# Reading Wv by rows and placing the expert weights' load behind the last normed rows' writes, in a gated attention and mixture-of-experts kernel

## The chip, the cores and the metric

The kernel runs on one core of a Trainium2 chip. The metric is the time of one execution in microseconds on the device. The kernel before takes 576.2 us in the median of three runs (575.97 to 576.66). A profiled execution of it took 577.64 us, of which 575.9 us lie between its first and its last instruction; all rows of the profile come from that execution.

## The reference, cut to what matters

The input x has 2 batches of 1024 tokens with 512 features, all in float32. Every row is normalised (layer norm without weights) to xn. Attention and a mixture of experts both start from xn, and their results are multiplied:

```
xn  = (x - mean) / sqrt(var + 1e-5)
q, k, v = split(xn @ w_qkv.T + b_qkv)            # 512 features each
s   = softmax(q @ k.T / sqrt(512)) @ v @ w_out.T + b_out
logits = xn @ router_w + router_b                 # 8 experts
top 2 experts per token, softmax over the two logits
f   = sum over the two: weight * silu(xn @ expert_w[e] + expert_b[e])
y   = xn + f @ proj_w + proj_b
g   = silu(norm_w * y / sqrt(mean(y*y) + 1e-6))
out = x + s * g
```

The host hands `w_qkv` and `w_out` over transposed, so that `w_qkvT` has a row for each input feature (512 rows) and 1536 columns; the last 512 columns are Wv.

## The kernel before, in words

Tokens are handled in 16 tiles of 128 rows. The features of a row are not kept in their natural order. VectorE transposes 32 by 32 blocks, and the kernel lays x, the weights and the normed rows out so that such block transposes are enough. The contraction over 512 features runs in four steps of 128, and step j takes the features q*128 + j*32 + b for q in 0..3 and b in 0..31. A weight that is contracted with xn must have its rows in the same order.

The work goes through these stages.

1. **Head.** Wv and Wo are multiplied into one matrix, so that values come out already projected: `wv_in` (Wv in four chunks of 128 rows) is transposed chunk by chunk on TensorE (`turn_wv`, L394), copied by VectorE into `wvT`, and multiplied with `wo` (`product_vo`, L403) for two halves n of the output columns and four row groups hc. Results land in `rwvo`, which also holds the eight columns of the router weights (`rw`). In between, statistics of the first x tiles are taken (`parts`, `means`, `variances`), x is normed by ScalarE in place (`norm`), transposed by VectorE (`turn_x`) and written to DRAM as `xn_d`, two tiles at a time in four DMAs (`store`, L381). `turn_w` transposes the blocks of Wq (`wZ[0]`) and of Wk (`wZ[1]`). `hold` (L220) issues matmuls on a constant tile whose result nobody reads.
2. **Values.** For t from 0 to 15, `value_half` multiplies xnT with `rwvo` (the `pv` matmuls, L457); each step of the loop also norms, stores or takes statistics of later tiles, and does one part of the weights' work. Logits come out of the same matmuls.
3. **Routing.** After the last tile the pools of the first stages are closed (`close(ln_guard)`), and their room goes to the routing tiles (`hsel`, `tsel`, `lsel`, L677 to L698) and to the expert biases `eb`. The two experts of each token are found, tokens are counted by expert, and 39 slots of 128 rows get their lists of tokens (`tok`). Meanwhile TensorE multiplies Wq and Wk (`product`) and the queries (`queries`, the `pq` matmuls, L549). It does `queries(0)` ahead of the token matmuls `ptok` (L706) and `queries(1)` to `queries(3)` behind them.
4. **Experts.** A pipeline over 39 slots: `gather` (POOL, an indirect DMA, L782) fetches a slot's rows of `xn_d` seven slots ahead, `put_s` writes them to DRAM in another layout (`xs`), `take_s` reads them back (`sz`), `turn_s` transposes them on VectorE (`gT`), and `expert` multiplies them with the expert's weights out of `ew` (the `ph` matmuls, L808). The expert's number is only known at run time, so the matmul depends on the whole tile `ew` (8 MB). Results are written by ACT's queue to `ho_d`.
5. **Attention and the gate**, in pairs of tiles, to the end.

The order on each engine is the written order: `keep_order()` ties every instruction to the one before it on its engine. DMAs are issued by SP in that order too, a few by ACT and POOL. In the built program every DMA that SP or ACT issues waits for the one eight DMAs earlier to have landed. A DMA of SP that has to wait keeps back everything behind it on SP.

The head's DMAs stand on SP in this order: Wv chunks 0 and 1, the first half of Wo, Wv chunks 2 and 3, x tiles 0 and 1, the second half of Wo, `wZ[0]`, x tiles 2 and 3, x tiles 4 to 15, `wZ[1]`. ACT issues the biases `bqkv` and then the router weights (four DMAs of 4 KB). At step t = 12 of the values' loop the `raw` pool is closed, and the 32 DMAs of `ew` are issued at once. Step t = 13 issues `store(14)`, the write of tiles 14 and 15, so it stands behind `ew` on SP.

Of the kernel before, what the change touches and what calls it, by code (L numbers as in the profile page):

```python
# [10 lines left out]
FP = mybir.dt.float32  # L11
# [9 lines left out]
P = 128  # L21
# [6 lines left out]
def kernel(  # L28
# [17 lines left out]
    B, S, H = hidden.shape  # L46
    E = router_w.shape[1]
    KC = H // P
# [18 lines left out]
    def pool(name, bufs=1, side="left", **where):  # L67
        guard = tc.tile_pool(name=name, bufs=bufs, side=side, reuse_waits="tile", **where)
        return guard, guard.__enter__()
# [3 lines left out]
    def close(guard):  # L73
        guard.__exit__(None, None, None)
# [25 lines left out]
    pe, dve, act, gps, sp = nc.tensor, nc.vector, nc.scalar, nc.gpsimd, nc.sync  # L100
# [8 lines left out]
    QP = P // 4  # L109
# [22 lines left out]
    def turn_w(dst, z):  # L132

        for r in range(KC):
            dve.transpose(
                dst.rearrange("p j (i q a) -> p i j q a", i=4, q=4)[:, :, :, r, :],
                z[:, ts(r, 4), :].rearrange("p i (j b) -> p i j b", b=QP),
            )
# [22 lines left out]
    raw_guard, raw = pool("raw", side="right")  # L161
# [12 lines left out]
    def load_x(t, n):  # L174
        for q in range(4):
            sp.dma_start(
                x[ts(q, QP), ds(t, n)].rearrange("p t i f -> p (t i) f"),
                xr_d[ds(t * P, n * P), ts(q, P)].rearrange("(n a) f -> a n f", a=QP),
            )

    wv_in = raw.tile([P, KC, H], FP, name="wv_in")
# [3 lines left out]
    bqk = const.tile([P, 2, KC], FP, name="bqk")  # L185

    def load_wv(c):
        sp.dma_start(
            wv_in[:, c, :],
            w_qkvT.rearrange("(q j b) o -> j q b o", q=4, b=QP)[c][:, :, ts(2, H)],  # L190
        )

    def load_wo(n):
        sp.dma_start(
            wo[:, :, ts(n, HH)], w_outT[:, ts(n, HH)].rearrange("(c p) h -> p c h", p=P)
        )

    act.dma_start(bqkv, b_qkv.rearrange("p (i c) -> p i c", i=3))
    load_wv(0)
    load_wv(1)  # L200
    load_wo(0)
    for c in range(2, KC):
        load_wv(c)
    load_x(0, 2)
    load_wo(1)
    spread(sp, wZ[0], w_qkvT[:, ts(0, H)])
    load_x(2, 2)
    for q in range(4):
        act.dma_start(
            rw[ts(q, QP), :, 0:E], router_w[ts(q, P), :].rearrange("(j b) e -> b j e", b=QP)  # L210
        )
    for t in range(4, NT, 4):
# [7 lines left out]
    def hold(n):  # L220
        ps = ps_mm.tile([P, 512], FP, tag="mm", name="hold")
        for _ in range(n):
            pe.matmul(ps[:, : 2 * P], lhsT=idle[:, 0:P], rhs=idle, start=True, stop=True)
# [92 lines left out]
    def weighted(w_, bias, name):  # L316

        s_ = raw.tile([P, H], FP, tag="s", name=name, bufs=3)
        for c in range(KC):
            b_ = bias[:, c : c + 1]  # L320
            if c:
                dve.scalar_tensor_tensor(s_, w_[:, c, :], b_, s_, ALU.mult, ALU.add)
            else:
                dve.tensor_scalar(s_, w_[:, c, :], b_, None, ALU.mult)
            yield s_
# [10 lines left out]
    def parts(t):  # L336
        for i in range(4):
            dve.bn_stats(st[:, t, i].rearrange("p h k -> p (h k)"), x[:, t, i, :])
# [10 lines left out]
    def means(t, n):  # L349
        g_ = ds(4 * t, 4 * n)  # L350
        at_ = st.rearrange("p t i h k -> p (t i) h k")[:, g_]
        dve.tensor_reduce(mean[:, g_], across(at_[:, :, :, 1], f"pmean{t}"), AX.X, ALU.add)
        dve.tensor_tensor(
            dev[:, g_],
            at_[:, :, :, 1],
            mean[:, g_].unsqueeze(2).to_broadcast([P, 4 * n, 2]),
            ALU.subtract,
        )
        dve.tensor_tensor(dev[:, g_], dev[:, g_], dev[:, g_], ALU.mult)
        dve.scalar_tensor_tensor(  # L360
            dev[:, g_], at_[:, :, :, 2], 8.0 / H, dev[:, g_], ALU.mult, ALU.add
        )

    def variances(t, n):
        g_ = ds(4 * t, 4 * n)
        dve.tensor_reduce(var[:, g_], across(dev[:, g_], f"pvar{t}"), AX.X, ALU.add)
        act.activation(std[:, g_], var[:, g_], AF.Sqrt, bias=ln_eps)
        dve.reciprocal(rstd[:, g_], std[:, g_])
        dve.scalar_tensor_tensor(
            shift[:, g_], mean[:, g_], -1.0, rstd[:, g_], ALU.mult, ALU.mult  # L370
        )

    def norm(t):
        for i in range(4):
            n = 4 * t + i
            act.activation(  # L376
                x[:, t, i, :], x[:, t, i, :], AF.Identity,
                bias=shift[:, n : n + 1], scale=rstd[:, n : n + 1],
            )

    def store(t):  # L381

        for q in range(4):
            sp.dma_start(
                xn_d[ds(t * P, 2 * P), ts(q, P)].rearrange("(n a) f -> a n f", a=QP),
                x[ts(q, QP), ds(t, 2)].rearrange("p t i f -> p (t i) f"),
            )

    def turn_x(t):
        turn(xnT[t // ST][:, :, ts(t % ST, P)], x[:, t], "(i a)")  # L390

    wvT = {}

    def turn_wv(c):  # L394
        ps = ps_mm.tile([P, 512], FP, tag="mm", name=f"wvt{c}").rearrange(
            "p (o f) -> p o f", o=KC
        )
        for oc in range(KC):
            pe.transpose(ps[:, oc, :], wv_in[:, c, ts(oc, P)], ident)
        wvT[c] = raw.tile([P, KC, P], FP, name=f"wvT{c}")  # L400
        dve.tensor_copy(wvT[c], ps)

    def product_vo(n, hc):  # L403
        at_, size = halves[n]
        ps = ps_mm.tile([P, 512], FP, tag="mm", name=f"pvo{hc}_{n}")
        for c in range(KC):
            pe.matmul(
                ps[:, :size],
                lhsT=wvT[hc][:, c, :],
                rhs=wo[:, c, ts(n, HH)],  # L410
                start=(c == 0),
                stop=(c == KC - 1),
            )
        act.copy(rwvo[:, hc, at_ : at_ + size], ps[:, :size])

    hold(12)
    turn_wv(0)
    hold(6)
    turn_wv(1)
    product_vo(0, 0)  # L420
    turn_wv(2)
    parts(0)
    parts(1)
    product_vo(0, 1)
    turn_wv(3)
    product_vo(0, 2)
    means(0, 2)
    product_vo(0, 3)
# [23 lines left out]
    def value_half(t, n):  # L452
        if t not in pvs:
            pvs[t] = ps_big.tile([P, 2, 512], FP, tag="big", name=f"pv{t}")
        cols = (ds(0, HH + E1), ds(HH + E1, HH))[n]
        for c in range(KC):
            pe.matmul(  # L457
                pvs[t][:, n, : HH + E1 * (1 - n)],
                lhsT=xnT[t // ST][:, c, ts(t % ST, P)],
                rhs=rwvo[:, c, cols],  # L460
                start=(c == 0),
                stop=(c == KC - 1),
            )

    def keep_values(t):
        pv = pvs.pop(t)
        dst = vo[t // ST][:, t % ST, :].rearrange("p (n f) -> p n f", n=2)
        act.copy(dst, pv[:, :, 0:HH])
        act.copy(lg1[:, t, :], pv[:, 0, HH : HH + E1])
# [25 lines left out]
    for t in range(2, NT):  # L495
        if 2 < t < NT - 1:
            turn_x(t + 1)
        value_half(t, 1)
        keep_values(t - 1)
        if t in (2, 5, 9):  # L500
            first = {2: 4, 5: 8, 9: 12}[t]
            means(first, 4)
        value_half(t, 0)
        if t in (2, 5, 9):
            variances(first, 4)
        if t + 2 < NT:
            norm(t + 2)
            if t % 2:
                store(t + 1)
        if 3 <= t < 7:  # L510
            parts(2 * t + 2)
            parts(2 * t + 3)
        if t == 2:
            gps.dma_start(bo, b_out.partition_broadcast(P))
        if t == 8:
            turn_w(wqkT[:, KC:], wZ[1])
        if t == 9:
            *_, sk_ = weighted(wqkT[:, KC:], bqk[:, 0], "sk")
        if t == 10:

            *_, vb = weighted(wo, bqkv[:, 2], "vb")
        if t == 11:
            dve.tensor_copy(u, columns(sk_, "pu"))
        if t == 12:
            pvb = ps_mm.tile([P, 512], FP, tag="mm", name="pvb")
            pe.matmul(pvb, lhsT=ones, rhs=vb, start=True, stop=True)
            dve.tensor_tensor(bo, pvb, bo, ALU.add)
            close(raw_guard)
            ew_guard, ewp = pool("ew", side="right")
            ew = ewp.tile([P, E, KC, H], FP, name="ew")  # L530
            for e in range(E):
                for q in range(4):
                    sp.dma_start(
                        ew[ts(q, QP), e],
                        expert_w[e, ts(q, P), :].rearrange("(j b) f -> b j f", b=QP),
                    )
# [159 lines left out]
    for g in range(2 * NT // LG):  # L696
# [7 lines left out]
        for j in range(LG):  # L704
# [3 lines left out]
                lhsT=lsel[:, j, :],  # L708
# [522 lines left out]
    for k in range(NP):  # L1231
# [43 lines left out]
        o = attend(k)  # L1275
# [81 lines left out]
```

## Time and profile before

| what | us |
|---|---|
| median of three runs | 576.2 (575.97 to 576.66) |
| profiled execution | 577.64 |
| its span | 575.9 |
| TensorE busy | 537.6 |
| VectorE busy | 310.7 |
| POOL busy | 215.7 |
| ScalarE busy | 167.5 |
| first `pv` matmuls with the logits' columns (L457) | 44.64 |
| first expert matmul (L808) | 171.66 |
| mean granted TensorE clock | 0.97 |

Times of events count from the span's start. A row of the chain of work that ended last gives start, length, engine, what was written and read, and its line. A row of stretches gives the stretch, its length, the busy time of TensorE's matmuls, TensorE's weight loads, VectorE, ScalarE and POOL (with counts of instructions), then the granted TensorE clock, the mean busy share of the 16 DMA engines, and what they moved in GB/s. A row of waits gives who waited, for whom, total, times and longest.

### The profile page before, as it was taken

Reading aid. Unit: us, or ns where it says so; the run is one execution under the profiler, and the core shown is the slowest. Engines: PE = TensorE matmul, PEld = TensorE weight load, DVE = VectorE, ACT = ScalarE, POOL = GpSimd, SP = SyncE. Lnnn points to the kernel's source line nnn. Section 1 sums busy time; section 2 is a strip of 40 time slices with the busy share of each in tenths; the row PEclk is TensorE's granted clock in tenths of the full one; section 3 lists DMA queues with packets and bytes.
Section 4 is the critical chain, followed back from the end, with each engine's and each line's share of the span. In section 5 each row is a group of like instructions: output and inputs, shape, how many; then the busy total and the mean of one; then the engine's idle time right before and its main releaser. Section 6 shows DMA issues by size and latency. Waiting matters only on the chain.

```text
span 575.9 us, 5914 instructions
## 1 busy us (share of the span) xinstructions
PE 537.6 (93%) x1758; PEld 327.1 (57%) x1758; DVE 310.7 (54%) x565; ACT 167.5 (29%) x316; POOL 215.7 (37%) x238
## 2 busy tenths in 40 slices
PE   5789999980899999999999999999999999999997
PEld 3568878630444444444446666675674847475486
DVE  0264763403403333433376846638479595868686
ACT  0143754210012111121134152242342425252340
POOL 6000000000342457632202744524819857484542
PEclk9997999995699999999999999999999999999999
DMA  5898225999498999999737792362532827365522
GB/s 122 181 213 162 71 71 117 211 211 252 132 325 254 274 334 349 303 303 302 220 143 242 232 314 70 105 242 73 184 146 74 306 94 275 128 219 204 179 92 75
DMA packets 95857, 112.38 MB, mean 195 GB/s; under 512 B 7248, under 2 KB 65744, under 8 KB 95696
## 3 DMA queue, kind: packets, MB, share of 16 engines
q1 hardware_dynamic: 83696, 82.86, 50.5%
q0 software_dynamic: 5792, 18.88, 10.4%
q10 hardware_dynamic: 6336, 10.25, 4.8%
q8 instruction: 15, 0.25, 0.2%
q14 instruction: 18, 0.15, 0.1%
HBM read 70.54 MB, written 41.42 MB: 194 GB/s over the span
## 4 chain that ended last, share of the span: by engine, by line
PE 76%; DMA 13%; DVE 7%; issue 2%; ACT 0%; SPq 0%; DVEq 0%
PE ph L808 19%; PE so L1141 16%; PE pp L1070 13%; PE po L1007 10%; PE pv L457 7%; DMA ew<-in_L_ffn_expert_w_dram 6%; PE pq L549 4%; PE pr L568 4%; DMA wv_in<-in_L_attn_w_qkv_dram 3%; PE sc L1051 2%; DMA wZ<-in_L_attn_w_qkv_dram 1%; DMA xn_d<-x 1%; DMA x<-_attn_hidden_states_dram 1%; DVE lsel L698 1%; DVE sc L1076 1%
## 5 line engine op out<-in xcount | busy, mean ns | idle before, releaser
L808 PE MATMUL ph<-ew,gT 128*128 x280 | 120.3, 592 | 0.0
L782 POOL DMA_INDIRECT xg<-xn_d,tok x39 | 37.2, 954 | 199.7 <-DVE npast L727 138.3
L808 PEld LDWEIGHTS ph<-ew,gT 128*128 128x128 f32 x280 | 53.2, 190 | 67.0 <-issue 67.0
L834 DVE TENSOR_TENSOR h<-ph,eb 128x512 f32<-128x512 f32 x39 | 26.9, 689 | 83.9 <-issue 55.3
L457 PE MATMUL pv<-rwvo,xnT 128*128 128x256 f32 (+1 forms) x256 | 62.3, 400 | 1.3 <-DVE xnT L120 1.0
L457 PEld LDWEIGHTS pv<-rwvo,xnT 128*128 128x128 f32 x256 | 49.5, 197 | 10.8 <-ACT x L376 1.4
L837 ACT ACTIVATE h<-h 128x512 f32<-128x512 f32 x39 | 24.6, 631 | 96.5 <-DVE h L834 96.5
L1007 PE MATMUL po<-pw,ct 128*128 128x512 f32 x112 | 49.2, 592 | 0.0
L1038 ACT ACTIVATE pr<-sc,nm 128x1024 f32<-128x1024 f32 x16 | 18.3, 1144 | 90.8 <-DVE nm L1035 89.1
L969 POOL DMA_INDIRECT hg<-ho_d,posi_m x32 | 31.7, 990 | 33.0 <-DMA ho_d<-h 22.3
L1148 DVE TENSOR_TENSOR o<-so,o 128x256 f32<-128x256 f32 x49 | 20.0, 421 | 39.2 <-PE so L1141 22.5
L1070 PE MATMUL pp<-xnT,qT 128*128 128x512 f32 x84 | 39.5, 592 | 0.0
L1186 POOL TENSOR_TENSOR o<-o,base 128x512 f32<-128x512 f32 x14 | 20.6, 1491 | 48.9 <-DVE o L1151 48.0
L1141 PE MATMUL so<-vo,pT 128*128 128x256 f32 x168 | 38.5, 379 | 0.0
L1141 PEld LDWEIGHTS so<-vo,pT 128*128 128x128 f32 x168 | 31.9, 190 | 7.3 <-issue 2.6
L1007 PEld LDWEIGHTS po<-pw,ct 128*128 128x128 f32 x112 | 21.3, 190 | 25.5 <-issue 25.4
L1076 DVE TENSOR_TENSOR sc<-pp,sc 128x512 f32<-128x512 f32 x49 | 31.6, 679 | 5.2 <-PE pp L1070 5.2
L549 PE MATMUL pq<-xnT,wqk 128*128 128x512 f32 x64 | 30.6, 636 | 0.0
L120 DVE STREAM_TRANSPOSE gT<-sz 128x512 f32<-128x512 f32 x39 | 27.4, 702 | 4.3 <-DMA sz<-xs 4.3
L568 PE MATMUL pr<-xnT,wqk 128*128 128x256 f32 x128 | 28.8, 381 | 0.9 <-DVE sc L1076 0.9
L120 DVE STREAM_TRANSPOSE pT<-pz 128x1024 f32<-128x1024 f32 x14 | 28.1, 2007 | 0.0
L568 PEld LDWEIGHTS pr<-xnT,wqk 128*128 128x128 f32 x128 | 24.2, 190 | 6.6 <-DVE sc L1076 2.2
(223 smaller groups left out, 792.3 us busy)
## 6 DMA issues: line engine op xcount, KB each, us to landing
xs<-xg SPq DMA_DIRECT2D x39, 256.0 KB
sz<-xs SPq DMA_DIRECT2D x39, 256.0 KB
ho_d<-h ACTq DMA_DIRECT2D x39, 256.0 KB
ew<-in_L_ffn_expert_w_dram SPq DMA_DIRECT2D x32, 256.0 KB
ps<-pr SPq DMA_DIRECT2D x16, 512.0 KB
pz<-ps SPq DMA_DIRECT2D x16, 512.0 KB
xn_d<-x SPq DMA_DIRECT2D x32, 128.0 KB
cs<-hg SPq DMA_DIRECT2D x16, 256.0 KB
```

Of the source, the lines that this page charges most:

```text
L120: dve.transpose(dst.rearrange(f"p j {order} -> p i j a", a=QP), z.rearrange("p i (j b) -> p i j b", b=QP),)
L457: pe.matmul(pvs[t][:, n, : HH + E1 * (1 - n)], lhsT=xnT[t // ST][:, c, ts(t % ST, P)], rhs=rwvo[:, c, cols], start=(c == 0), stop=(c == KC ...
L549: pe.matmul(ps[:, half, :], lhsT=wqk[:, c, ts(oc, P)], rhs=xnT[0][:, c, ts(half, 512)], start=(c == 0), stop=(c == KC - 1),)
L568: pe.matmul(ps[:, :PW], lhsT=wqk[:, c, ts(oc, P)], rhs=xnT[1][:, c, ts(k, PW)], start=(c == 0), stop=(c == KC - 1),)
L782: gps.indirect_dma_start(out=xg[s], out_offset=None, in_=xn_d, in_offset=bass.IndirectOffsetOnAxis(ap=tok[:, s : s + 1], axis=0),)
L808: pe.matmul(ph, lhsT=g_[:, c, :], rhs=ew[:, ds(r, 1), c, :].rearrange("p e f -> p (e f)"), start=(c == 0), stop=(c == KC - 1),)
L834: dve.tensor_tensor(h, ph, eb[:, ds(r, 1), :].rearrange("p e f -> p (e f)"), ALU.add)
L969: gps.indirect_dma_start(out=g_, out_offset=None, in_=ho_d, in_offset=bass.IndirectOffsetOnAxis(ap=posi_m[:, n, t : t + 1], axis=0),)
L1007: pe.matmul(po, lhsT=c_[:, c, :], rhs=pw[:, c, :], start=(c == 0), stop=(c == KC - 1))
L1070: pe.matmul(ps, lhsT=l_[:, c, :], rhs=r_[:, c, :], start=(c == 0), stop=(c == KH - 1))
L1076: dve.tensor_tensor(dst, ps, other, ALU.add)
L1141: pe.matmul(ps[:, :w_], lhsT=l_[:, c, :], rhs=r_[:, c, :], start=(c == 0), stop=(c == SK - 1),)
```

## The change

Four things move.

- A chunk of Wv is now 128 neighbouring rows of `w_qkvT`, not four groups of 32 rows. The four chunks are loaded first, ahead of Wo.
- The order of features is made when a transposed chunk is copied: `wvT` becomes one tile, and the copy of chunk c writes runs of 32 elements into it. A product then reads from all four chunks, so all four are transposed ahead of the first product, with four more `hold` matmuls behind them.
- The router weights' four DMAs go from ACT's queue to SP's, behind x tiles 2 and 3.
- The pool of `ew` is opened, and its DMAs are issued, at step t = 13 and not at t = 12. `store(14)` then stands ahead of them on SP.

```diff
     def load_wv(c):
-        sp.dma_start(
-            wv_in[:, c, :],
-            w_qkvT.rearrange("(q j b) o -> j q b o", q=4, b=QP)[c][:, :, ts(2, H)],
-        )
+        sp.dma_start(wv_in[:, c, :], w_qkvT[ts(c, P), ts(2, H)])
...
     act.dma_start(bqkv, b_qkv.rearrange("p (i c) -> p i c", i=3))
-    load_wv(0)
-    load_wv(1)
+    for c in range(KC):
+        load_wv(c)
     load_wo(0)
-    for c in range(2, KC):
-        load_wv(c)
     load_x(0, 2)
     load_wo(1)
     spread(sp, wZ[0], w_qkvT[:, ts(0, H)])
     load_x(2, 2)
     for q in range(4):
-        act.dma_start(
+        sp.dma_start(
             rw[ts(q, QP), :, 0:E], router_w[ts(q, P), :].rearrange("(j b) e -> b j e", b=QP)
         )
...
-    wvT = {}
+
+    wvT = raw.tile([P, KC, KC, 4, QP], FP, name="wvT")
...
-        wvT[c] = raw.tile([P, KC, P], FP, name=f"wvT{c}")
-        dve.tensor_copy(wvT[c], ps)
+        dve.tensor_copy(wvT[:, :, :, c, :], ps.rearrange("p o (j b) -> p o j b", b=QP))
...
-                lhsT=wvT[hc][:, c, :],
+                lhsT=wvT[:, c, hc].rearrange("p q b -> p (q b)"),
...
     turn_wv(0)
     hold(6)
     turn_wv(1)
+    turn_wv(2)
+    turn_wv(3)
+    hold(4)
     product_vo(0, 0)
-    turn_wv(2)
     parts(0)
     parts(1)
     product_vo(0, 1)
-    turn_wv(3)
     product_vo(0, 2)
...
             dve.tensor_tensor(bo, pvb, bo, ALU.add)
             close(raw_guard)
+        if t == 13:
             ew_guard, ewp = pool("ew", side="right")
             ew = ewp.tile([P, E, KC, H], FP, name="ew")
             for e in range(E):
```

## The prediction

> **What bounds the kernel now.** I read the time slices first, then the chain that ended last, then the waits of VectorE, then stretches of the time line with their DMA share and granted clock.
>
> ```profile
> PE   5789999980899999999999999999999999999997
> ...
> PEclk9997999995699999999999999999999999999999
> ```
>
> Each digit is 14.4 us. TensorE is below nine tenths in two places, slices 1 to 3 and slices 9 to 11; behind them it is full. A change in the first 172 us must act in one of these two.
>
> ```profile
> 0.82 7.34 DMA wv_in<-in_L_attn_w_qkv_dram
> ...
> 8.17 12.77 DMA wv_in<-in_L_attn_w_qkv_dram
> 20.96 8.34 DMA wZ<-in_L_attn_w_qkv_dram
> 29.32 5.59 DMA x<-_attn_hidden_states_dram
> ...
> 122.69 9.90 DMA ew<-in_L_ffn_expert_w_dram
> 132.61 5.75 DMA xn_d<-x
> ...
> 138.59 1.50 DVE hsel L677
> ...
> 171.66 109.88 PE ph L808 x256
> ```
>
> In the chain (start, length, what) the head hangs on four loads of Wv, the last landing at 20.96, then on wZ and x. The second gap hangs on the expert weights `ew`, behind which the last four writes of normed rows `xn_d` stand; `hsel` takes the room of x and so waits until these writes have read it.
>
> ```profile
> DVE hsel L677 <- DMA xn_d<-x: 22.1, 1, 22.1
> ...
> PE wvt L399 <- DMA wv_in<-in_L_attn_w_qkv_dram: 7.0, 3, 4.4
> ```
>
> The columns are total, times and longest: VectorE waited 22.1 us at one place, TensorE 7.0 us in three waits.
>
> ```profile
> 2.20:8.20 6.00, 1.72 (x9) 0.91 (x6) 0.00 (x0) 1.28 (x1) 5.04 (x34) 1.00 0.57 125
> 8.20:20.96 12.76, 9.59 (x34) 6.65 (x34) 2.08 (x3) 0.74 (x2) 2.98 (x12) 1.00 0.71 170
> 20.96:44.64 23.68, 19.05 (x87) 15.95 (x87) 12.66 (x45) 8.72 (x21) 0.00 (x0) 0.91 0.97 203
> 96.40:135.50 39.10, 30.43 (x96) 17.32 (x94) 8.65 (x32) 6.81 (x13) 0.00 (x0) 0.92 1.07 213
> 129.20:144.20 15.00, 0.00 (x0) 0.00 (x1) 5.58 (x5) 0.00 (x0) 0.00 (x0) 0.50 0.91 249
> 157.00:171.50 14.50, 14.50 (x37) 6.50 (x36) 1.71 (x4) 2.23 (x2) 6.47 (x7) 1.00 1.02 325
> 171.66:292.00 120.34, 120.34 (x284) 53.25 (x284) 44.60 (x69) 23.85 (x36) 50.13 (x48) 1.00 0.93 289
> ```
>
> The last three columns are clock, DMA share and GB/s. The DMA engines have room while Wv comes (0.57, 0.71) and none while `ew` comes (1.07); the expert loop needs 289 GB/s.
>
> **The change part by part.**
>
> *Wv by rows.* The same 256 KB a chunk and 2 KB a row, but 128 rows in one run and no four groups of 32. The first chunk took 7.34 us; the nearest load of the new shape, `sz` (128 rows of 2 KB), was issued at 157.04 and ended VectorE's wait at 160.46: 3.4 us, beside other traffic. So chunk 0 lands at 0.82 + 3.4 = 4.2, not 8.16.
>
> The Trainium skill (DMA: Bandwidth & Descriptors, section "Why a DMA increments its semaphore by 16 and not by 1") gives a reason: a DMA is spread over the largest count of engines up to 16 that divides the outermost dimension longer than one on both sides, here 4 before and 16 after. The low DMA share beside a late chunk agrees; the sum would be the same by rule and by row.
>
> *Order of the first products.* A product now reads all four copied chunks; before, the first two chunks let the first product start at 12.82. In TensorE's order: transposes of chunk 0 and six hold matmuls, 2.4 us as measured from 8.29 to 10.66; three more chunks at 1.1 us (0.63 at full clock); four hold matmuls, 4/6 of 1.49 = 1.0. From 4.2 that ends at 10.9. The copies write runs of 32 elements in place of 512; no row shows this on the same operation, so I take 0.69 us, the old copy with the same elements and source, under the hold matmuls; at twice that the last copy costs 0.4 (1.4 against 1.0), at less nothing is gained. The first half of Wo is there: 1.57 MB from 2.2 us at 203 GB/s is 9.9. Three products at 1.89 end at 16.6. The first two x tiles: 2.10 MB at 203 GB/s from 2.2 is 12.5, their statistics (1.65) 14.2, so they no longer hold the means (before, VectorE waited for them until 23.20). Mean, fourth product and variance matmul take 2.7 at full clock: 19.3 against 28.41 now. All behind is arithmetic in the same order, 16.2 us to the pv matmuls at 44.64 (the chain goes over the load of x to 34.90, but VectorE's transposes of x ended at 34.96, so the load was not the later one). Next in line is wZ and the second half of Wo: 1.57 MB more, 20.3, wanted at 34.9 - 9.1 = 25.8; then x of tiles 2 and 3, 22.9, wanted at 28. So 9.1 us off. Ends: one product at half clock (3.75, the row at 12.82) leaves 7.2; transposes at full clock give 10.9; x at only 125 GB/s (2.2 to 8.2) leaves 5. I take 9.
>
> *Router weights on SP.* Four issues of together 2.47 us move from ACT's queue to SP's, behind x tiles 2 and 3 and ahead of x tiles 4 to 15 and wZ[1]. ACT's first copy waits for TensorE anyway: nothing. Tiles 4 to 7 land near 22.9 + 5.2 + 2.5 = 30.6, wanted at 45.12 - 9 = 36: covered; without the cover it costs 2.5. The weights themselves land near 26, wanted by 35.
>
> *Expert weights behind the writes.* Times here are still those of before; all slides by the 9. Tile 15 is normed at 96.38; the writes' four issues take 1.83 (as at 87.70), so `ew` is issued from 98.2, not 95.05, behind a wait of SP for ACT that delays nothing but `ew`. The writes land near 101, so `hsel` starts when VectorE is ready, 116.5, not 138.59. Selections (1.5 + 2.9 + 4.6) end by 125.6, under the queries that hold TensorE to 126.83. Token matmuls at full clock 1.5, the rest as measured 1.4: the first gather at 130 against 149.76. TensorE goes on: 126.83 + 1.5 + 7.03 + 0.2 + 13.8 = 149.4.
>
> What is late next: the gathered rows. On SP's queue `xs` stands behind `ew` and `eb`, in order. `ew` 8.39 MB at 213 GB/s: 98.2 + 1.3 + 39.4 = 138.9; four gathers beside it, 1.05 MB at 325, up to 3.2 more: 142.1; `eb` 2.10 MB at 350 GB/s (139 to 145 now): 148.1. First `xs` 149.5, `sz` 3.4 more, transpose 0.7: the first expert at 153.6, TensorE idle 4.2. Now TensorE went idle at 126.83, the clock read 0.50 from 129.2, and the sixteen `pq` matmuls at 148.1 took 9.58 for the 7.03 of those at 119.8: an idle stretch costs 0 to 2.5; I take 1.5. That gives 171.66 - 155.1 = 16.5 us. Ends: no idle time, 22.2; rows late by one more put and take (7.2, from 153.22 to 160.46) with the full clock price make 163.3, so 8.4.
>
> The skill's clock rule (TensorE: Matmul & The Clock Gate, section "Part 1: The HAM clock gate (the 'warmup' mystery)") has the clock halved after an idle window of about 3.4 us and restored after as long a busy one; it speaks against this order, and by it the idle 4.2 would cost up to 1.7. The row of 129.2 agrees with its direction.
>
> *Sum.* 9 + 16.5 = 25.5 us. The profiled execution took 577.64 (span 575.9 and 1.7 around it): 552.1. The median is 576.2, 1.4 lower: 550.7, say 551.
>
> **The rivals.**
> *Fully covered:* rows arrive before 149.4, because the gathers do not slow `ew`. Gain 9 + 22.2: 545. For it, `ew` moves 213 GB/s where `eb` moves 350, so the engines' own rate is not its limit and gathers may cost it less than 3.2; against it, the DMA share of 1.07.
>
> *Late rows, or a loop paced by DMA:* now eleven gathers are issued before the first expert and VectorE never waits for `sz` after 163.24; after the change the loop starts with nothing in hand. Up to the 35th slot it moves 36.4 MB from 148.1 on (35 slots of gather, put and take at 0.79 MB, 34 results at 0.26, `proj_w` 1.05, less the four gathers done); at 325 GB/s done at 260, before TensorE wants it (153.6 + 34 x 3.43 = 270), below 298 GB/s not. Gain 9 + 8.4: 559.
>
> *The head stays:* chunks land as late as now or the products wait for all four: gain 16.5 alone, 560. Against it, 3.4 us for the same shape.
>
> *The writes free nothing:* another reader of that room holds `hsel`: gain 9, 567. Against it, the wait names only these writes.
>
> *Slower:* the loop paced by DMA throughout. Its 36.4 MB would have to take 25.5 us beyond 270, so below 247 GB/s, against 305 to 355 from 190 to 220. A little under that, 580.
>
> **How the numbers follow.** Forecast 0.48, covered 0.12, late rows 0.20, head stays 0.10, nothing freed 0.05, slower 0.04, no change 0.01. From 544 to 561 holds the first four, 0.90, less what falls beyond their edges. A measurement tells 0.2% (1.2 us) from no change: faster 0.95, same 0.01, slower 0.04.
>
> **What would show it.** Chunk 0 landing near 4 and pv in full run near 36; no wait of `hsel` for `xn_d`; first gather near 121 and first expert near 145 (both less 9); a wait of VectorE for the first `sz`. Wrong: repeated waits for `sz` inside the loop, a half clock for more than one window behind the first expert, or pv still near 44.

## The result, and the profile after

The changed kernel takes 549.84 us in the median of four runs (549.26 to 552.6). The kernel before takes 576.09 (575.47 to 576.66, four runs). The ratio is 0.9552, with a 95% interval of 0.9523 to 0.9581. The forecast was 551, with a range of 544 to 561. The profiled execution of the changed kernel took 552.6 us, the longest of its four; its span is 550.9, so the span fell by 25.0.

The time slices of the changed kernel (one digit is now 13.8 us):

```profile
PE   7889999999699999999999999999999999999996
...
PEclk9979999999899999999999999999999999999999
DMA  9995336999999999998468732812823728285512
```

The two low places of before are almost gone. Slices count from 1, as in the prediction. What is left of the first place are the digits 7, 8 and 8 in slices 1 to 3 and a clock of 7 in slice 3 (27.5 to 41.3 us). Of the second only slice 11 (137.7 to 151.5 us) is left.

The chain that ended last, of the changed kernel, around the two places:

```profile
2.67 6.86 DMA wo<-in_L_attn_w_out_dram
...
10.29 10.45 DMA wZ<-in_L_attn_w_qkv_dram
...
119.41 9.28 DMA xg<-xn_d,tok
128.71 10.77 DMA xs<-xg
139.63 2.91 DMA sz<-xs
142.56 0.72 DVE gT L120
143.32 63.89 PE ph L805 x144
...
268.03 13.73 PE sc L1048 x32
```

No wait for a load of Wv stands in it, and no `hsel`. The second place now hangs on the first gathered rows: the gather (9.28 us), its put (10.77) and its take (2.91). The first expert starts at 143.32, where it was 171.66.

The waits of the changed kernel (total, times, longest):

```profile
DVE gT L120 <- DMA sz<-xs: 23.7, 5, 17.1
...
PE ph L805 <- DVE gT L120: 5.4, 2, 4.4
...
DVE h L831 <- DMA ho_d<-h: 5.1, 1, 5.1
```

In the same stretch VectorE's wait of `hsel` is down from 22.1 us to 0.2. VectorE now waits for the gathered rows (`sz`), but 4.4 us, ahead of the first expert, is all that TensorE notices of it. TensorE's other wait for `gT` (0.96 us near 207 us) is not due to the rows: VectorE stood there for 5.1 us until the write of an earlier result (`ho_d`) had landed, and came to `gT` late.

The time line of the changed kernel, head and routing (start, length, engine, line, what, and in brackets the idle time before and its releaser):

```profile
3.71 0.78 PE L395 MATMUL wvt<-ident,wv_in 128*128 128x128 f32 x4
...
9.66 5.42 PE L402 MATMUL pvo<-wo,wvT 128*128 128x256 f32 x24 [1.64 <-DMA wo<-in_L_attn_w_out_dram]
...
16.87 0.29 PE L339 MATMUL pvar<-dev,eighth 128*128 128x16 f32 x2
...
28.06 3.61 PE L453 MATMUL pv<-rwvo,xnT 128*128 128x256 f32 x8
...
34.81 7.23 PE L453 MATMUL pv<-rwvo,xnT 128*128 128x265 f32 x24 [0.26 <-DVE rwvo L477]
...
88.57 33.20 SPq L530 DMA_DIRECT2D ew<-in_L_ffn_expert_w_dram  x32
106.72 1.49 DVE L674 TENSOR_TENSOR hsel<-iota,hi 128x1280 bf16<-128x1280 f32 x1 [0.22 <-DMA ew<-in_L_ffn_expert_w_dram]
```

Chunk 0 is transposed from 3.71 (8.29 before), and the variance matmul ends at 17.16 (28.41 before). That is 11.2 us earlier, but the `pv` matmuls with the logits' columns start only 9.8 earlier, 34.81 against 44.64.

Stretches of the changed kernel (busy times, then clock, DMA share, GB/s):

```profile
2.20:8.20 6.00, 4.94 (x35) 3.75 (x32) 2.55 (x4) 0.33 (x1) 4.89 (x34) 1.00 0.99 292
27.90:36.50 8.60, 6.85 (x26) 5.71 (x27) 5.42 (x21) 1.95 (x5) 0.00 (x0) 0.70 1.22 219
88.60:122.00 33.40, 33.40 (x128) 18.66 (x127) 19.15 (x48) 6.78 (x13) 2.00 (x2) 1.00 1.04 218
138.90:143.30 4.40, 0.00 (x0) 0.00 (x0) 0.71 (x1) 1.11 (x1) 2.47 (x3) 1.00 0.78 212
143.30:146.50 3.20, 3.18 (x5) 1.42 (x6) 0.71 (x1) 0.00 (x0) 1.31 (x2) 0.61 0.90 305
160.00:220.00 60.00, 59.03 (x138) 25.81 (x137) 22.71 (x35) 11.19 (x18) 36.49 (x33) 1.00 1.01 320
```

While Wv and the loads behind it come, the DMA engines are full (0.99 and 292 GB/s, against 0.57 and 125). The 1.4 us lost in the head lie in the second row: at a clock of 0.70 the eight `pv` matmuls at 28.06 took 3.61 us, where eight took 1.97 at 39.23 before. The third row is the load of `ew`. The fourth row is TensorE's idle stretch, the fifth the low clock behind it. The loop is not paced by DMA (last row: TensorE busy 59 of 60 us).

The 25.0 us of span add up as follows.

| part | before | after | difference |
|---|---|---|---|
| start to the `pv` matmuls with the logits' columns | 44.64 | 34.81 | -9.83 |
| from there to the first expert | 127.02 | 108.51 | -18.51 |
| first expert to the first `sc` matmul | 121.40 | 124.71 | +3.31 |
| from there to the end | 282.8 | 282.9 | 0 |

Of the +3.31, 1.7 are the low clock (3.2 us at 0.61 and 3.5 us at 0.87 cost 1.25 and 0.45), and 0.96 is the wait for `gT` near 207 us. The rest lies in no row that I can name.

### The profile page after: what moved, and what is told of

Read it like the earlier page. It is cut to its first block, busy times and chain, and to the rows that moved or that the text cites. A ratio compares the mean times of both kernels' runs of the same rounds, so it can differ in the third digit from the quotient of the medians.

```text
span 550.9 us, 5922 instructions
## 1 busy us (share of the span) xinstructions
PE 530.7 (96%) x1762; PEld 323.5 (59%) x1762; DVE 310.9 (56%) x565; ACT 167.4 (30%) x316; POOL 216.5 (39%) x238
## 3 DMA queue, kind: packets, MB, share of 16 engines
q0 software_dynamic: 5792, 18.88, 10.9%
## 4 chain that ended last, share of the span: by engine, by line
PE 82%; DMA 8%; DVE 6%; issue 2%; ACT 1%; SPq 0%; DVEq 0%
PE ph L805 20%; PE so L1138 17%; PE pp L1067 14%; PE po L1004 10%; PE pv L453 9%; PE pr L565 4%; PE sc L1048 2%; PE pqk L577 2%; DMA xs<-xg 2%; DMA wZ<-in_L_attn_w_qkv_dram 2%; DMA xg<-xn_d,tok 2%; PE pq L546 1%; DMA wo<-in_L_attn_w_out_dram 1%; DVE sc L1073 1%; DVE pT L120 1%
## 5 line engine op out<-in xcount | busy, mean ns | idle before, releaser
L805 PE MATMUL ph<-ew,gT 128*128 x280 | 122.5, 600 | 5.4 <-DVE gT L120 5.4
L453 PEld LDWEIGHTS pv<-rwvo,xnT 128*128 128x128 f32 x256 | 49.8, 199 | 10.8 <-ACT x L371 1.4
L546 PE MATMUL pq<-xnT,wqk 128*128 128x512 f32 x64 | 28.1, 594 | 0.0
```

The costliest lines, as they stand in the source:

```text
L453: pe.matmul(pvs[t][:, n, : HH + E1 * (1 - n)], lhsT=xnT[t // ST][:, c, ts(t % ST, P)], rhs=rwvo[:, c, cols], start=(c == 0), stop=(c == KC ...
L546: pe.matmul(ps[:, half, :], lhsT=wqk[:, c, ts(oc, P)], rhs=xnT[0][:, c, ts(half, 512)], start=(c == 0), stop=(c == KC - 1),)
L805: pe.matmul(ph, lhsT=g_[:, c, :], rhs=ew[:, ds(r, 1), c, :].rearrange("p e f -> p (e f)"), start=(c == 0), stop=(c == KC - 1),)
```

## The experiments

Diffs are against the changed kernel, save for the second experiment, which is against the kernel before. "Loop" is the time from the first expert to the first `sc` matmul, 121.40 in the kernel before. Each ratio is against runs of the kernel before made in the same set (medians 574.68 to 577.07 us), so across experiments the ratios compare better than the times.

### The head alone: expert weights issued at t = 12 again

```diff
-        if t == 13:
             ew_guard, ewp = pool("ew", side="right")
```

> The changed kernel with one part undone: the expert weights' loads stand again ahead of the last four writes of normed rows. Theory (two gains, one in the head and one in the routing, which add): the pv matmuls with the logits' columns stay at 34.8 us, the wait of hsel for the writes is back and ends near 138.6 - 9.8 = 128.8, the first expert starts near 161.8, and the time is 576.1 - 9.8 = 566.3 us. Rival (the head's gain is swallowed later, the whole gain is in the routing): hsel still starts near 138.6 and the time is near 576.

Measured: 564.54 us, ratio 0.9773 (0.9732 to 0.9813); the span of 565.1 is 10.8 below before. Its chain and its waits:

```profile
128.68 1.50 DVE hsel L673
...
160.84 109.88 PE ph L804 x256
```

```profile
DVE hsel L673 <- DMA xn_d<-x: 21.8, 1, 21.8
```

The wait of `hsel` is back, 21.8 us for the 22.1 of before, only 9.9 earlier. The loop is again 121.40. So the head part alone gives its ten microseconds, and with all the rest of the change in place the wait still hangs on the place of the expert weights.

### The expert weights alone

```diff
+        if t == 13:
             ew_guard, ewp = pool("ew", side="right")
```

> The kernel before with one part alone: the expert weights' loads behind the last writes. Theory: pv stays at 44.6 us, hsel starts near 116.5, the first expert near 143.3 + 9.8 = 153.1, the loop costs the 3.3 us more that the changed kernel's costs, and the time is 576.1 - 15.2 = 560.9 us. Rival (the routing's gain needs the earlier head): less than 10 us gained, above 566.

Measured: 561.23, ratio 0.9716 (0.9672 to 0.9760); the span of 560.3 is 15.6 below before. Its chain:

```profile
129.60 9.69 DMA xg<-xn_d,tok
139.31 10.98 DMA xs<-xg
...
154.03 111.84 PE ph L809 x256
```

The three numbers of the changed kernel's second place are here without the new head: a gather of 9.7, a put of 11.0, and a first expert 17.6 earlier than before. `hsel` waits for no write (0.2 us). The 256 expert matmuls took 111.84 against 109.88, so a low clock behind an idle stretch (5.0 us of idle time here, then a clock of 0.51 for 3 us) costs 2.0. By spans the two parts alone give 10.8 + 15.6 = 26.4, together 25.0. By ratios it is 5.1% (give or take 0.6) against 4.5% (0.3). They are close to independent.

### The old shape of the chunks in the new order

```diff
-        sp.dma_start(wv_in[:, c, :], w_qkvT[ts(c, P), ts(2, H)])
+        sp.dma_start(
+            wv_in[:, c, :],
+            w_qkvT.rearrange("(q j b) o -> j q b o", q=4, b=QP)[c][:, :, ts(2, H)],
+        )
...
-        dve.tensor_copy(wvT[:, :, :, c, :], ps.rearrange("p o (j b) -> p o j b", b=QP))
+        wvT[c] = raw.tile([P, KC, P], FP, name=f"wvT{c}")
+        dve.tensor_copy(wvT[c], ps)
```

> The changed kernel with Wv's chunks as before (four groups of 32 rows, plain copies), all else as changed: the four loads first, four transposes ahead of the products, router weights on SP, expert weights behind the writes. Theory (the shape of a chunk made its load slow): the fourth chunk lands past 13 us, the first product starts past 14 and not at 9.7, pv at 40 to 47, time 555 to 562 us. Rival (the order of the loads and the router weights' move gave the head's gain): pv stays near 35 and the time near 550.

Measured: 563.29, ratio 0.9738 (0.9686 to 0.9791); on the scale of the kernel before that is 561.0, at the upper end of what was expected. Its time line:

```profile
18.63 1.09 PE L398 MATMUL wvt<-ident,wv_in 128*128 128x128 f32 x4 [3.14 <-DMA wv_in<-in_L_attn_w_qkv_dram]
20.38 6.80 PE L406 MATMUL pvo<-wo,wvT 128*128 128x256 f32 x24
```

The last chunk is transposed at 18.63 and not at 6.96, in 2.2 to 8.2 us the DMA share is 0.31, and `pv` with the logits' columns starts at 46.89, 2.2 us later than before the change. All of the head's gain hangs on the shape of the load. With the old shape, the new order gives nothing; most of the 2.2 us that it loses here is again a slow group of eight `pv` matmuls (3.62 us for 1.97).

### The router weights on ACT's queue again

```diff
-        sp.dma_start(
+        act.dma_start(
             rw[ts(q, QP), :, 0:E], router_w[ts(q, P), :].rearrange("(j b) e -> b j e", b=QP)
         )
```

> The changed kernel with the router weights' four DMAs on ACT's queue as before. Theory (that move costs and gives nothing): pv at 34.8 us within 1, time 549.8 within 1 us. Rival (the small DMAs at the start take places among the eight in flight and hold back Wv and Wo): the first product 2 us later than 9.7 or more, time 552 to 554.

Measured: 548.54, ratio 0.9514 (0.9465 to 0.9564), a little below what was expected. A row of its time line, and the stretch behind its idle time:

```profile
8.96 5.45 PE L402 MATMUL pvo<-wo,wvT 128*128 128x256 f32 x24 [0.55 <-DVE wvT L396]
```

```profile
140.10:143.50 3.40, 3.38 (x4) 1.45 (x5) 0.54 (x1) 0.00 (x0) 1.41 (x2) 0.52 0.89 298
```

The first product and the `pv` matmuls (34.09) start 0.7 earlier, and the first expert at 140.12, 3.2 earlier: the first put took 6.56 us and not 10.77, and why is not shown. The interval overlaps the changed kernel's, so the times tell no difference; the move to SP is worth nothing, or costs a little. TensorE idled for only 2.1 us here, and still the clock read 0.52 behind it and the 256 expert matmuls took 111.84 us.

### The expert biases on ACT's queue

```diff
-    sp.dma_start(eb, expert_b.partition_broadcast(P))
+    act.dma_start(eb, expert_b.partition_broadcast(P))
```

> The changed kernel with the expert biases' load (2 MB) issued by ACT's queue and no longer by SP's between the expert weights and the first xs. Theory (the first rows wait on SP's queue behind the biases): the biases come beside the expert weights, xs lands 4 us earlier or more, VectorE's wait for the first sz ends near 139, TensorE does not idle ahead of the first expert, time 543.5 to 546.5. Rival (the rows are late because the gathers and all else share full DMA engines, in whatever order): first expert near 143 as in the changed kernel, time 549 to 551.

Measured: 561.99, ratio 0.9770 (0.9709 to 0.9831): the expectation missed. Its time line and its waits:

```profile
122.40 0.34 ACTq L539 DMA_DIRECT2D eb<-in_L_ffn_expert_b_dram  x1
122.77 1.28 ACT L614 ACT_TABLE_LOAD   x1 [26.38 <-DMA ew<-in_L_ffn_expert_w_dram]
```

```profile
PE pq L546 <- ACT wqk L584: 14.7, 1, 14.7
```

The program lets a DMA of ACT start only when the one eight issues earlier has landed, and those are the `ew` loads of SP. So ACT stood for 26.38 us with the copies of `wqk` behind it, and TensorE waited 14.7 us for these. The edit measured this new wait and could not tell what it was made for.

### Biases behind the first rows on SP

```diff
-    sp.dma_start(eb, expert_b.partition_broadcast(P))
...
+        if s == -3:
+            sp.dma_start(eb, expert_b.partition_broadcast(P))
```

> The changed kernel with the biases' load on SP as before but behind the first sz. Theory (the first rows wait behind the biases): VectorE's wait for the first sz ends near 137 and the first expert starts when the queries end, near 138.9; then the second or third slot's rows wait behind the biases for 1 to 4 us; time 545 to 549. Rival (order does not matter, only bytes): first expert near 143, 550.

Measured: 551.75 (546.06 to 552.11), ratio 0.9577 (0.9504 to 0.9650); 545 to 549 was expected. Two rows of its chain, then two of its time line:

```profile
128.57 4.73 DMA xs<-xg
...
134.78 10.38 DMA sz<-xs
```

```profile
138.85 3.60 PE L804 MATMUL ph<-ew,gT 128*128 x8
145.95 18.47 PE L804 MATMUL ph<-ew,gT 128*128 x36 [3.50 <-DVE gT L120]
```

The first put took 4.73 us and not 10.77, and the first expert follows the queries without a gap, as expected. But the second slot's rows now stand behind the biases: its take took 10.38 us instead of 2.9, and TensorE waited 3.50 one slot later. The idle time moved by a slot. No difference to the changed kernel can be told from the times.

### Biases on POOL's queue, and with the router weights on ACT's

```diff
-    sp.dma_start(eb, expert_b.partition_broadcast(P))
+    gps.dma_start(eb, expert_b.partition_broadcast(P))
```

> The changed kernel with the biases' load issued by POOL, which is idle until the gathers and waits for no loads of expert weights. Theory (the first rows wait on SP's queue behind the biases; what made the load on ACT slow was ACT's wait for loads of expert weights): the biases move beside the expert weights from about 97, the weights end up to 6 us later, near 130, xs lands near 133, the wait for the first sz ends near 137, the first expert starts when the queries end, near 139, the clock stays at 1.00, the loop costs 121.4 to 122.5 us and the time is 544 to 546.5. Rival (bytes, not order: all must pass the same full engines ahead of the first rows): first expert at 142 to 144, time 548.5 to 551.

Measured: 551.48, ratio 0.9562 (0.9538 to 0.9586): the theory missed and its rival holds. The biases went out at 91.93, amid the issues of `ew`; these ended later (127.96 for 121.77), the first put took 10.34 us and the first expert started at 143.78. A stretch of it:

```profile
96.00:119.00 23.00, 23.00 (x89) 11.19 (x88) 17.24 (x41) 5.50 (x9) 0.00 (x0) 1.00 1.03 248
119.00:128.00 9.00, 9.00 (x24) 4.10 (x23) 2.10 (x11) 1.11 (x1) 3.91 (x4) 1.00 1.08 212
```

The DMA share stays above 1 in both stretches. The rows are late by the bytes that are ahead of them in full DMA engines, whatever queue these come from.

The same with the router weights on ACT's queue as in the fourth experiment:

> The same with the router weights' four DMAs back on ACT's queue. Theory (that move costs up to 0.8 us in the head, and the rest of what its undoing gained was the xs behind the biases): 0.5 to 1 us below the kernel with only the biases on POOL. Rival (its undoing gains 2 us by itself): 2 us below.

Measured: 551.04 (549.12 to 555.02), ratio 0.9568 (0.9539 to 0.9597). By the times there is no gain over the biases on POOL alone, which speaks against the 2 us that the fourth experiment's median seemed to show. The profile, of the fastest of its six runs, has an earlier head all the same (`pv` at 32.28, where the run above has 35.26):

```profile
8.73 5.42 PE L402 MATMUL pvo<-wo,wvT 128*128 128x256 f32 x24 [0.85 <-DMA wo<-in_L_attn_w_out_dram]
...
27.06 1.97 PE L453 MATMUL pv<-rwvo,xnT 128*128 128x256 f32 x8
```

### The changed kernel once more

> The changed kernel itself once more, on the same chip as the two others, so that their differences of 1 to 5 us can be read: 0.955 of the kernel before, first expert between 140 and 146.

Measured: 552.91, ratio 0.9582 (0.9558 to 0.9606). A row of its chain:

```profile
144.88 111.94 PE ph L805 x256
```

Gather 9.47 us, put 11.35, first expert 144.88, TensorE's wait 5.3: the same picture in another set of runs. There is no second wait for `gT`, and the loop is 123.45, so it lost 2.0 us and not 3.3. The two ratios of one kernel, 0.9552 and 0.9582, show how little a difference of 0.3% between these experiments means.

### Holding the clock through the idle stretch

Behind the queries, 32 `hold` matmuls that nobody reads:

```diff
+    hold(32)
```

> The changed kernel with 32 matmuls on a constant tile between the last queries and the first expert, about 3.4 us of the 4.4 us in which TensorE idled; their result is read by nobody. Theory (the idle stretch halves the clock and that costs 1.5 to 1.7 us): first expert where it was, clock 1.00 in the 3.2 us behind it and not 0.61, time 548.1. Rival (the loop's longer time is waits for sz): 549.8, within 0.6.

Measured: 550.99, ratio 0.9578 (0.9526 to 0.9629). The rows came 3 us later in its profile (first expert at 146.22), so TensorE was idle for 2.97 us once the hold matmuls were through at 143.25, and the clock read 0.50 from 146.5 to 150. The experiment did not reach its condition and does not say whether a clock held up would pay.

### Half of the expert weights

```diff
-            for e in range(E):
+            gps.memset(ew[:, E // 2 :], 0.0)
+            for e in range(E // 2):
```

> The changed kernel with the weights of experts 4 to 7 set to zero by POOL and not loaded, so this part of the computation is left out: 4.2 MB less stand ahead of the first rows. Theory (the first rows are late because all bytes ahead of them pass full DMA engines, whatever their order): the engines are free by about 117, the first gather lands 3 to 4 us after its issue and not 9, VectorE's wait for the first sz ends before 133, TensorE goes from the queries into the first expert near 139 with no idle time, the clock stays at 1.00 and the loop costs 121.4 us as in the kernel before; time 542.5 to 545.5. Rival (the late rows come from the gather, put and take steps themselves): first expert at 142 to 144, 548 to 551. Second rival (the loop's 2 to 3 us more are DMA pacing, not the idle start): first expert near 139 but the loop still 123 to 125 us.

The weights of experts 4 to 7 are set to zero and not loaded, so the kernel leaves out what these experts compute; TensorE does as many matmuls as before, and 4.2 MB less come ahead of the rows.

Measured: 544.86 (543.26 to 545.15), ratio 0.9454 (0.9412 to 0.9495). Its chain, a row of its time line, and a stretch:

```profile
139.07 109.88 PE ph L806 x256
```

```profile
122.99 3.79 SPq L112 DMA_DIRECT2D xs<-xg  x3
```

```profile
119.00:128.00 9.00, 9.00 (x24) 4.16 (x23) 1.79 (x10) 1.11 (x1) 4.07 (x5) 1.00 0.63 163
```

With the DMA share at 0.63 and not above 1, the gather issued at 119.60 landed in 3.4 us, not 9.3. The first expert followed the queries without idle time, the 256 matmuls took 109.88 us, and the loop was 121.40. This settles the second place: the late rows, the idle stretch and the low clock behind it come from the weights that are still under way. The wait of 0.96 us near 207 us, for the write of a result, is not shown to come from them; the second measurement of the changed kernel has none. By the ratios (0.9454 against 0.9552 and 0.9582) all that costs 1.0 to 1.3%, 5.6 to 7.4 us.

### Eight of the weights' loads ahead of the writes

```diff
-        if t == 13:
             ew_guard, ewp = pool("ew", side="right")
             ew = ewp.tile([P, E, KC, H], FP, name="ew")
-            for e in range(E):
+        if t in (12, 13):
+            for e in range(2) if t == 12 else range(2, E):
```

Two of the eight experts' weights (8 DMAs, 2.1 MB) are issued at t = 12, then the writes, then the other 24 DMAs.

> The changed kernel with the first eight of the 32 loads of expert weights issued at step 12 again, the last normed rows' writes behind them, the other 24 loads behind the writes. Theory (bytes ahead of the rows through full engines; SP and the engines idle from 85 to 88.6): the writes land near 99, still ahead of the 106.5 at which VectorE comes to hsel, the weights end 3.5 us earlier, the first expert starts at 139.5 to 140.5, time 3 to 5 us below the changed kernel, 545 to 548. Rival (the writes now land too late, past 106.5, or the eight in flight hold SP back): hsel waits for the writes, the first expert is no earlier, 550 or more.

Measured: 546.25 in the median of six runs (545.08 to 549.36), ratio 0.9492 (0.9456 to 0.9528). That interval lies below the one of the changed kernel's second measurement (0.9558 to 0.9606), and reaches the lower end of its first (0.9523 to 0.9581) by 0.0005. Its time line, waits and stretches:

```profile
87.05 4.08 SPq L530 DMA_DIRECT2D ew<-in_L_ffn_expert_w_dram  x8
91.23 3.17 SPq L379 DMA_DIRECT2D xn_d<-x  x4
95.45 25.01 SPq L530 DMA_DIRECT2D ew<-in_L_ffn_expert_w_dram  x24
...
141.73 38.86 PE L805 MATMUL ph<-ew,gT 128*128 x89 [0.85 <-DVE gT L120]
```

```profile
PE ph L805 <- DVE gT L120: 1.1, 2, 0.9
```

```profile
139.00:143.00 4.00, 3.15 (x8) 1.24 (x7) 1.29 (x2) 1.11 (x1) 3.02 (x4) 1.00 0.98 310
```

The weights' bytes begin at 87.05, though the head of this profiled execution was 1.8 us later than the changed kernel's (`pv` at 36.65), whose weights began at 88.57: 3.4 us earlier by the head. `hsel` still waits for nothing longer than 0.2. TensorE's wait for `gT` falls from 5.4 to 1.1 us, ahead of the first expert from 4.4 to 0.9, and the clock stays at 1.00. The first expert starts at 141.73, or 139.9 by the changed kernel's head, as expected. The first `sc` matmul comes at 264.33 instead of 268.03, and the span is 547.2. This version has the lowest ratio of those that compute everything; its interval overlaps that of the run with the router weights on ACT's queue (0.9465 to 0.9564).

## Why the prediction was right

The mechanism came out as forecast in both places, and the time (549.84 for 551) and the profiled time (552.6 for 552.1) within the terms' own errors. That they came so near is in part luck: the head gave 0.8 us more than taken and the routing 1.3 less, and two measurements of the same changed kernel (ratios 0.9552 and 0.9582) lie 1.7 us apart. Step by step:

- **Chunk 0 at 4.2:** landed by 3.71. The row of `sz` was the right one to price a load of 128 rows. The Trainium skill (DMA: Bandwidth & Descriptors, section "Why a DMA increments its semaphore by 16 and not by 1") would have four engines for the old shape and sixteen for the new; the DMA shares of 0.31 with four loads of the old shape in a row and of 0.99 with the new one agree with it (four of sixteen are 0.25).
- **First product at 10.9:** 9.66. The transposes of chunk 0 took 0.78 us, not 1.09; Wo was then late by 1.6 us, landing at 9.53 where I had 9.9. The copies in runs of 32 took 0.69 us, the value taken.
- **Variance matmul at 19.3:** 17.16. **Arithmetic of 16.2 behind it:** it took 17.65, since a low clock cost 1.4 us. The forecast had priced this stretch as before, with no change of the clock. The earlier start alone does not bring the low clock: in two other profiles of the new head (the one with the biases on POOL and the router weights on ACT, and the one with half the weights) the same eight matmuls took 1.97 us. Net, 9.8 us for the 9 taken.
- **Router weights on SP, nothing:** the times show no cost. In the profiles the first product starts at 9.60 to 10.18 us in all nine with the new head and these weights on SP's queue, and at 8.96 and 8.73 in the two with them on ACT's, so the move seems to cost the head about a microsecond. What it delays is not shown.
- **`hsel` no longer waits:** 0.2 us instead of 22.1. **First gather near 121:** 119.41. **First expert near 144.6:** 143.32.
- **What is late next:** the gathered rows, with 4.2 us of idle time: 4.4. The forecast had the biases landed at 139.1 and the first put at 140.5, then 3.4 for the take. The put landed at 139.5 (128.71 and 10.77) and the take took 2.9. That the put waits for bytes ahead of it is borne out by the run with the biases behind the first rows, where it took 4.73 us. It need not be the biases that stand last: with them on POOL's queue, landed by 104.4, and the end of `ew` later for it, the put took 10.34. What the forecast did not have is the gather's 9.28 us. It does not seem to have set the time: in the second measurement the gather had landed at 129.6 and the biases only at 140.2, just ahead of the put at 140.9.
- **Clock price 1.5:** this is the term of the routing that was too small. The low clock cost 1.7, but the loop lost 3.3 in all, 0.96 of it in the wait for `gT` that the write of a result brought. In six other profiles with an idle stretch, those whose chain has all 256 expert matmuls in one row, these took 111.59 to 113.12 us for 109.88, so 1.7 to 3.2 more, and the price did not grow with the idle time: 2.0 for 2.1 us, 1.7 for 5.8. Routing gave 18.5 - 3.3 = 15.2 us for the 16.5 taken. The Trainium skill's clock rule (TensorE: Matmul & The Clock Gate, section "Part 1: The HAM clock gate (the 'warmup' mystery)") halves the clock after an idle window of about 3.4 us and restores it after as long a busy one; the estimate from it is up to 1.7. That agrees with the 1.7 here, but the clock of 0.52 behind 2.1 us of idle time, with the router weights on ACT's queue, came after less than such a window.
- **Signs of being wrong:** VectorE did wait for `sz` four more times inside the loop, 1.2 to 2.1 us each, but no matmul waited for these.

The rivals. *Fully covered* (545) is what the kernel does with half the weights left out: 544.86. The 4.4 us of idle time and the low clock behind it keep the real one from it. *A loop paced by DMA* did not come: 320 GB/s, TensorE busy 59 of 60 us. *The head stays* is shown to be the price of the old chunk shape (563.29, or 561.0 by its ratio, for which I had 560). *Nothing freed* fell with the wait of `hsel`, and *slower* with the loop that DMA does not pace.

## What to carry to other kernels

Look at the DMA share where an engine waits for a load: a late load beside idle DMA engines asks for another shape of the load, and a late one beside full engines asks for fewer bytes ahead of it, on whatever queue. A write that frees room is short work that a long load must not stand ahead of; but the load has its own deadline behind it, so put as much of the load ahead as the write can bear. Before an issue is moved to another queue, find what that queue's next DMA waits for.

## What the runs showed of the hardware that was not expected

- An indirect gather of 256 KB on POOL's queue took 9.0 to 11.2 us in seven profiles, from its issue to the first put behind it, while `ew` was under way (a DMA share of 1.07 in the changed kernel's second profile), and 3.4 us at a share of 0.63 with half the weights. The prediction had priced the gathers by what they add to the weights, not by what the weights add to them.
- Full DMA engines do not mean the same rate. At a share of 1.04 the `ew` loads moved 218 GB/s. From 129 to 136 us, when the biases and the rows moved, it was 355 GB/s at 1.07.
- The first matmuls' speed differs between executions, of one program too, though the clock in the profiles reads 1.00 there. In the kernel before, four transposes took 1.09 us until 12 us and 0.63 from 16.57; in the changed one the first four took 0.78 us in one profile and 1.09 in the other, and those behind them 0.63 or less.
- In the stretch from 27.9 to 36.5 us the changed kernel is the slower one: a clock of 0.70, for 0.96 in the matching stretch before. TensorE had waited there 1.9 us for statistics of x. That wait alone does not set the clock: twelve profiles with the new order of the head have it, 1.85 to 1.88 us long, and the eight matmuls behind it took anything from 1.97 to 3.62 us. What decides it is open.
- The clock can fall behind a short idle stretch: 2.1 us without a matmul were followed by a clock of 0.52 for 3.4 us, and cost as much as stretches of 5 us did (111.84 us for 256 matmuls in both).
